# First block of a two-block transformer on one core: where half products, norms and turns stand in the order of the cycles

## The chip, the cores and the metric

The kernel runs on one core of one Trainium2 chip. The metric is the device time of one execution in microseconds (us); lower is better. A core has five engines that run in parallel, each through a queue of its own in order: TensorE (PE in the profile, with its weight loads as PEld), VectorE (DVE), ScalarE (ACT), GpSimd (POOL), and SyncE (SP), which here only issues DMA transfers. PE writes its results to PSUM, which has eight banks of 128 partitions by 512 floats. A second PE product can only go into a bank when the engine that reads the first one has read it.

## The reference, cut to what matters

Two transformer blocks follow each other on x of 8 batches, 512 tokens and 256 features, all in float32. The change touches the first block only:

```python
# 16 heads of 16 features, scale = 16 ** -0.5
h = modulate(ln(x), shift_sa, scale_sa)
q = ln(_heads(h, H)) * qn_w + qn_b
k = ln(_heads(h, H)) * kn_w + kn_b
v = _heads(h, H)
attn = softmax(q @ k.T * scale)                    # 512 x 512 for each head
x = x + gate_sa * unheads(attn @ v)
h = modulate(ln(x), shift_ca, scale_ca)
q = heads(h @ wq.T + bq)                           # keys and values from 64 context tokens
x = x + gate_ca * (unheads(softmax(q @ k.T * scale) @ v) @ ca_out_w.T + ca_out_b)
h = modulate(ln(x), shift_ff, scale_ff)
x = x + gate_ff * (silu(h @ w1.T) * (h @ w3.T)) @ w2.T   # 1024 hidden features
```

The second block (self-attention, cross-attention and a feed-forward with 64-wide heads) follows for all batches.

## The kernel before, in words

**Order by hand.** The first block is written with every engine's order fixed by the program: whatever a function emits stands in each engine's queue in the order of the calls. What differs from one build to the next is only which PSUM bank (`bank()`, L75, eight of them) a product gets.

**Stages and cycles.** Three classes hold the work of one batch: SelfAttention (`norm` L493, `centre`, `square`, `var`, `scale` L533 to L553, `heads_turned` L560, `queries_keys` L575, `score` L598, `value` L606, `back` L630), CrossAttention (`prepare` L677, `turn`, `blocks`, `queries` , `score` L705, `value` L712, `inverse` L726, `scaled` L729, `out` L734) and FeedForward (`prepare` L742, `up` L757, `down` L774). `beginning` (L797) runs batch 0's self-attention. Then `cycle(c)` (L841) runs for c = 1 to 7: self-attention of batch c (`s`), parts of the norm of batch c+1 (`nxt`), cross-attention of batch c-1 (`x`), the upper half of the feed-forward of batch c-2 (`up`), and the output product of cross-attention c-2 (`done`) and the lower half of feed-forward c-3 (`down`). `ending` (L875) finishes. In cycle 1 the keys of the second block's cross-attention (`keys1`, L929) are computed beside it, two rounds of products for each pair.

**Groups.** A cycle has four groups of self-attention, g = 0 to 3, of four heads each, and one of cross-attention between groups 2 and 3. `group` (L787) puts them in order:

```python
for fn in (*scores[:2], *beside, *scores[2:], *short, *values, *rest):
    fn()
```

A score for one block of 128 keys is four matmuls of 16 rows, one in each quarter of the PE array, so that they can run at the same time; each writes a bank of its own. ACT takes the exponentials (L655) into `p` tiles, of which there are 14; a group needs 16. The values are sixteen matmuls that add up in one bank. So a pair of scores fills all eight banks, and the next products wait for exponentials.

**Turns.** Queries and keys need the heads along partitions, and the values have to come back to tokens. There are two ways for both. On PE: four transposes against the identity (L591 for queries and keys, L638 in `back`), after ACT has copied the values from their bank (L625). By blocks: DVE transposes blocks of 32 by 32 (L564 in `heads_turned`, L617 in `value`, L413 in `blocks_turned`) and DMA writes the blocks to DRAM and reads them back in order (L567 to L572: six transfers; L621 to L623: five). `by_blocks` (L627) chooses for the values: every batch but the first, and not the last group of the last batch.

**Norms.** `norm(0)` and `norm(1)` take the statistics of two of four tiles each on DVE and end with a power on POOL (L158); `norm(2)` scales four tiles on DVE (L191, `ln`) and modulates them on POOL (L509, L511). `inverse` (L727) is one reciprocal of 128 by 512 on DVE, `scaled` (L731) multiplies with it and also calls `check` (L125), two reductions that only watch the range of numbers.

## Time and profile before

| what | value |
|---|---|
| runs | 2304.17 us median (2301.11 to 2304.48) |
| profiled execution, own time | 2307.33 us |
| its span | 2305.5 us |
| mean granted clock of PE | 0.989 |
| PE, DVE, ACT, POOL busy | 2269.9, 1161.9, 849.9, 883.2 us |
| cycle 1, first scores to the next cycle's first scores | 78.46 to 152.67 us |
| cycles 2, 3, 4 | from 152.67, 239.97, 331.67 us |
| cycle 7, to its last values | 605.05 to 693.39 us |

The span is that of the instructions on the core; the time of an execution includes what lies around it. A line of the timeline gives start, length, engine, line, operation, tiles (written<-read) and count, and in brackets the idle time ahead with what ended it. PE counts one float32 matmul as two records, a transpose as one. Line numbers are those of the kernel before; `ps_B` is a bank of the first block, L88 the helper through which all matmuls go. PEclk is the share of PE's full clock that was granted.

Of the kernel before, what the change touches and what calls it, by code (L numbers as in the profile page):

```python
# [10 lines left out]
F32 = mybir.dt.float32  # L11
# [33 lines left out]
def fast_path(ctx: ExitStack, tc: tile.TileContext, a: dict, out: bass.AP):  # L45
# [437 lines left out]
    class SelfAttention:  # L483
# [143 lines left out]
        def by_blocks(self, g):  # L627
            return self.b > 0 and (self.b, g) != (B - 1, 3)
# [43 lines left out]
    class CrossAttention:  # L672
# [56 lines left out]
        def scaled(self, c):  # L729
            s = self.s  # L730
            nc.vector.tensor_tensor(s["oT", c], s["oT", c], s["den", c], ALU.mult)  # L731
            check(s["den", c])
# [4 lines left out]
    class FeedForward:  # L737
# [19 lines left out]
        def up(self, f):  # L757
            s = self.s
            if f == 0:
                s["hid"] = wk3.tile([P, 8, N], F32, tag="hid", name="hid", bufs=1)  # L760
            fs = slice(f * P, (f + 1) * P)
            pss = []
            for w in (w_1, w_3):
                ps = bank()
                for k in range(2):
                    mm(ps, w[:, k, fs], s["hT"][:, k, :], k == 0, k == 1)
                pss.append(ps)

            t = wk3.tile([P, N], F32, tag="t", name="t")
            nc.scalar.activation(t, pss[0], AF.Tanh, scale=0.5)  # L770
            nc.vector.scalar_tensor_tensor(t, t, 1.0, pss[0], ALU.add, ALU.mult)
            nc.vector.tensor_tensor(s["hid"][:, f, :], pss[1], t, ALU.mult)

        def down(self, qp):  # L774
            project_out(qp, lambda k: self.s["hid"][:, k, :], w_2, 8, add_gated(wk2, self.b, self.s["gate"]))

# [64 lines left out]
    def cycle(c):  # L841
# [4 lines left out]
        keys = [lambda p=p: keys1(p) for p in range(NPAIR)] if c == 1 else [lambda: None] * NPAIR  # L846
        store = store_keys1 if c == 1 else lambda g: None
        late = [up.turn] if c == 2 else []
        soon, then = ([x.turn], []) if c == 1 else ([], [x.turn])
        rows2, rows3 = ([] if c < n else [s.blocks] for s, n in ((x, 2), (up, 3)))  # L850

        scores, values = of_self(s, 0)
        group(scores, [keys[0], keys[1], lambda: done.out(0), lambda: done.out(1), lambda: up.prepare(0), lambda: up.prepare(1),
                       lambda: down.down(0), lambda: up.prepare(2), *rows3],
              [lambda: s.queries_keys(1), lambda: prev.back(3), lambda: nxt.norm(0), lambda: nxt.norm(1)], values, late)
        scores, values = of_self(s, 1)
        group(scores, [keys[2], lambda: store(0), lambda: s.heads_turned(1), lambda: down.down(1), lambda: x.prepare(0),
                       lambda: x.prepare(1), *([up.turn] if c > 2 else []), lambda: up.up(0), lambda: x.prepare(2), keys[3],
                       lambda: up.up(1), *rows2],
              [lambda: s.queries_keys(2), lambda: s.back(0), *soon, lambda: nxt.norm(2)], values)  # L860
        scores, values = of_self(s, 2)
        group(scores, [keys[4], *then, lambda: store(1), lambda: up.up(2), lambda: nxt.centre(0), lambda: up.up(3),
                       lambda: nxt.square(0), lambda: x.queries(0), lambda: x.queries(1)],
              [lambda: s.queries_keys(3), lambda: s.back(1), lambda: nxt.var(0), lambda: nxt.scale(0)], values)
        group([lambda: x.score(0), lambda: x.score(1)],
              [keys[5], lambda: up.up(4), keys[6], lambda: up.up(5), lambda: s.back(2), lambda: nxt.heads_turned(0),
               lambda: nxt.centre(1)], [], [lambda: x.value(0), lambda: x.value(1)])
        scores, values = of_self(s, 3)
        group(scores, [keys[7], lambda: store(2), lambda: x.inverse(0), lambda: up.up(6), lambda: x.scaled(0), lambda: nxt.square(1),
                       lambda: up.up(7)],  # L870
# [1501 lines left out]
```

### The profile page before, as it was taken

To read this page: it belongs to the slowest core of one execution; us is meant where nothing else is said; L and a number is where in the kernel's file an instruction comes from. 1 tells how busy PE (TensorE), PEld (TensorE's weight loads), DVE (VectorE), ACT (ScalarE), POOL (GpSimd) and SP (SyncE) were. 2 spreads that over 40 slices of the span, in tenths; PEclk is the share of its full clock that TensorE was granted. 3 is DMA by queue.
4 is the path that set the end of the run, shared out by engine and by line. 5 is a ranking of instruction groups with operands and counts; after the bars stand their busy time and mean duration, and the time that the engine had idled before them with its cause. 6 is when DMAs were issued, how large, how long until landed. Compare 5 with 4: busy or idle time off the path is not lost.

```text
span 2305.5 us, 30615 instructions
## 1 busy us (share of the span) xinstructions
PE 2269.9 (98%) x11880; PEld 1130.7 (49%) x11880; DVE 1161.9 (50%) x2018; ACT 849.9 (37%) x1282; POOL 883.2 (38%) x552
## 2 busy tenths in 40 slices
PE   9899999999999999999999999999999899999999
PEld 4333544535535543444444444444445456567666
DVE  5765765666555535444444445454444666642220
ACT  4555455464552123333333333333332121321221
POOL 4553333233211036555454545454544433320110
PEclk9999999999999999999999999999999999999999
DMA  6233313223220201111111111111032445442221
GB/s 192 56 110 97 76 47 87 75 50 89 58 68 31 66 1 46 26 29 29 29 29 29 29 29 29 29 26 32 20 88 83 105 104 121 93 102 56 56 62 36
DMA packets 148586, 139.62 MB, mean 61 GB/s; under 512 B 41009, under 2 KB 115489, under 8 KB 148433
## 3 DMA queue, kind: packets, MB, share of 16 engines
q1 hardware_dynamic: 147568, 134.96, 23.2%
q8 instruction: 95, 1.56, 0.3%
q0 software_dynamic: 576, 2.10, 0.2%
q10 hardware_dynamic: 288, 0.52, 0.1%
q14 instruction: 59, 0.48, 0.1%
HBM read 99.19 MB, written 38.35 MB: 60 GB/s over the span
## 4 chain that ended last, share of the span: by engine, by line
PE 91%; DVE 4%; DMA 3%; issue 1%; POOL 1%; SPq 1%; ACT 0%; DVEq 0%; POOLq 0%; ACTq 0%
PE ps_P L88 41%; PE ps_B L88 30%; PE ps_X L88 7%; PE ps_S L88 6%; PE ps_D L88 5%; PE ps_O L88 3%; DMA rb<-rec 1%; DMA turned_d<-hT 1%; DMA rec<-rec 0%; DVE p L1379 0%; DVE z L191 0%; DVE ln L191 0%; POOL var L557 0%; DVE t L911 0%; DVE hT L413 0%
## 5 line engine op out<-in xcount | busy, mean ns | idle before, releaser
L655 ACT ACTIVATE p<-ps_B 128x512 f32<-128x512 f32 x576 | 290.6, 629 | 201.9 <-PE ps_B L88 201.8
L1102 ACT ACTIVATE p<-ps_P 128x1024 f32<-128x1024 f32 x256 | 244.8, 1025 | 89.4 <-PE ps_P L88 89.4
L88 PE MATMUL ps_P<-q,k 32*128 32x512 f32 x2048 | 238.9, 600 | 1.4 <-DVE t L1081 1.4
L88 PE MATMUL ps_B<-hT,w 128*128 128x512 f32 x512 | 230.1, 604 | 0.9 <-ACT hT L407 0.9
L1111 POOL TENSOR_TENSOR sm<-sm,p 128x1024 f32<-128x1024 f32 x64 | 177.2, 2769 | 135.1 <-ACT p L1102 134.4
L88 PE MATMUL ps_P<-p,v 128*32 128x512 f32 x2048 | 226.4, 594 | 0.0
L158 POOL TENSOR_TENSOR rstd<-rstd,mhalf 128x4 f32<-128x4 f32 x49 | 52.4, 1069 | 325.9 <-DVE rstd L157 324.5
L1111 DVE TENSOR_TENSOR sm<-sm,p 128x1024 f32<-128x1024 f32 x64 | 102.0, 1594 | 145.0 <-ACT p L1102 145.0
L1070 ACT COPY v<-ps_P 128x1024 f32<-128x1024 f32 x32 | 32.4, 1012 | 377.0 <-PE ps_P L88 377.0
L88 PE MATMUL ps_B<-q,k 16*128 16x512 f32 x1024 | 156.1, 620 | 11.8 <-DVE oT L617 10.4
L88 PEld LDWEIGHTS ps_P<-q,k 32*128 32x128 f32 x2048 | 99.1, 184 | 139.2 <-issue 113.6
L88 PEld LDWEIGHTS ps_B<-hT,w 128*128 128x128 f32 x512 | 96.4, 192 | 129.1 <-issue 101.4
L88 PEld LDWEIGHTS ps_P<-p,v 128*32 128x32 f32 x2048 | 63.3, 110 | 158.3 <-issue 134.8
L557 POOL TENSOR_TENSOR var<-var,mhalf 128x32 f32<-128x32 f32 (+1 forms) x17 | 87.8, 5162 | 132.9 <-DVE var L551 132.9
L1109 POOL TENSOR_TENSOR sm<-p 128x1024 f32<-128x1024 f32 x32 | 79.1, 2471 | 152.7 <-ACT p L1102 152.7
L1080 DVE TENSOR_TENSOR t<-ps_P,rope_c 128x1024 f32<-128x1024 f32 x64 | 78.4, 1225 | 106.7 <-POOL q L1084 64.5
L88 PE MATMUL ps_B<-p,h 128*32 128x512 f32 x1024 | 131.7, 596 | 0.0
L1109 DVE TENSOR_TENSOR sm<-p 128x1024 f32<-128x1024 f32 x32 | 39.2, 1225 | 171.9 <-ACT p L1102 171.9
L88 PE MATMUL ps_P<-hT,w_sa_wq 128*128 128x512 f32 x256 | 118.4, 605 | 0.8 <-issue 0.8
L88 PE MATMUL ps_B<-w,hid 128*128 128x256 f32 x512 | 118.2, 391 | 0.0
L88 PE MATMUL ps_P<-hT,w_sa_wk 128*128 128x512 f32 x256 | 115.1, 592 | 0.0
L88 PE MATMUL ps_P<-w_sa_wv,hT 128*128 128x512 f32 x256 | 114.9, 592 | 0.0
(253 smaller groups left out, 3553.9 us busy)
## 6 DMA issues: line engine op xcount, KB each, us to landing
z<-turned_d SPq DMA_DIRECT2D x35, 512.0 KB
rb<-rec_d SPq DMA_DIRECT2D x64, 256.0 KB
rb<-rec SPq DMA_DIRECT2D x32, 512.0 KB
turned_d<-hT SPq DMA_DIRECT2D x104, 128.0 KB
back_d<-oT SPq DMA_DIRECT2D x108, 64.0 KB
oT<-back_d SPq DMA_DIRECT2D x27, 256.0 KB
turned_d<-sm SPq DMA_DIRECT2D x36, 128.0 KB
out_dram<-x SPq DMA_DIRECT2D x15, 256.0 KB
```

The costliest lines, as they stand in the source:

```text
L88: nc.tensor.matmul(o, lhsT, rhs, start=start, stop=stop)
L158: nc.gpsimd.tensor_tensor(r[:, :n], r[:, :n], mhalf[:, :n], ALU.pow)
L557: nc.gpsimd.tensor_tensor(var, var, half, ALU.pow)
L655: nc.scalar.activation(p[i], ps, AF.Exp, scale=HD0 ** -0.5)
L1070: nc.scalar.copy(s["v", half][:, t0 : t0 + 2, :], ps)
L1080: nc.vector.tensor_tensor(c, ps, rope_c[:, None, :].to_broadcast([P, 2, N]), ALU.mult)
L1102: nc.scalar.activation(pr, pss[u], AF.Exp, scale=HD1 ** -0.5)
L1109: eng.tensor_tensor(s["sm", g, u], s["p", g, 0, u], s["p", g, 1, u], ALU.add)
L1111: eng.tensor_tensor(s["sm", g, u], s["sm", g, u], s["p", g, kt, u], ALU.add)
```

## The change

Cycle 1 gets a list of its own without feed-forward work. In it batch 1's values and the queries and keys of groups 2 and 3, and of batch 2's groups 0 and 1, are turned on PE: `by_blocks` now begins with batch 2, and the two `heads_turned` of cycle 1 are gone. x.turn stays in group 1, and var(1) and scale(1) of batch 2 stay in group 3.

In the other cycles:
- `up` is split into gate_half (w_1, tanh, product on DVE) and value_half (w_3 and the last product). The value half of up(1) and of up(7) moves between second scores and values.
- down(0) becomes two tiles: the first stands directly behind the first scores of group 0, the second between second scores and values. Each has its own product with the gate and sum, 128 by 256.
- x.queries(1) moves between second scores and values of group 2.
- norm(0) and norm(1) (group 0), norm(2) (group 1), var(0) and scale(0) (group 2) move from ahead of the values to behind them.
- inverse(1) of cross-attention moves from group 3 to the next cycle's group 0, behind the first scores; scaled(1) follows the first tile of down, then var(1) and scale(1), then out(0) and out(1). The checks are taken out of `scaled` into `checked` and stand behind up.prepare(1).
- In cycle 7 inverse(1), scaled(1) and the checks stand behind the last values.

```diff
         def by_blocks(self, g):
-            return self.b > 0 and (self.b, g) != (B - 1, 3)
+            return self.b > 1 and (self.b, g) != (B - 1, 3)
...
         def scaled(self, c):
             s = self.s
             nc.vector.tensor_tensor(s["oT", c], s["oT", c], s["den", c], ALU.mult)
-            check(s["den", c])
+
+        def checked(self, c):
+            check(self.s["den", c])
...
         def up(self, f):
+            self.gate_half(f)
+            self.value_half(f)
+
+        def half(self, f, w):
+            ps = bank()
+            for k in range(2):
+                mm(ps, w[:, k, f * P : (f + 1) * P], self.s["hT"][:, k, :], k == 0, k == 1)
+            return ps
+
+        def gate_half(self, f):
             s = self.s
...
+            ps = self.half(f, w_1)
+            s["t"] = t = wk3.tile([P, N], F32, tag="t", name="t")
+            nc.scalar.activation(t, ps, AF.Tanh, scale=0.5)
+            nc.vector.scalar_tensor_tensor(t, t, 1.0, ps, ALU.add, ALU.mult)
+
+        def value_half(self, f):
+            s = self.s
+            nc.vector.tensor_tensor(s["hid"][:, f, :], self.half(f, w_3), s["t"], ALU.mult)
...
+        def down_tile(self, t):
+            ps = bank()
+            project_tile(ps, 0, lambda k: self.s["hid"][:, k, :], w_2, 8, t)
+            tmp = wk2.tile([P, 2, D], F32, tag="tmp", name="tmp", bufs=1)
+            x = xs[self.b][:, t, :]
+            nc.vector.tensor_tensor(tmp[:, 0, :], ps[:, 0:D], self.s["gate"], ALU.mult)
+            nc.vector.tensor_tensor(x, x, tmp[:, 0, :], ALU.add)
...
+        if c == 1:
+            scores, values = of_self(s, 0)
+            group(scores, [keys[0], keys[1]],
+                  [lambda: s.queries_keys(1), lambda: prev.back(3), lambda: nxt.norm(0), lambda: nxt.norm(1)], values)
+            scores, values = of_self(s, 1)
+            group(scores, [keys[2], lambda: store(0), lambda: x.prepare(0), lambda: x.prepare(1), lambda: x.prepare(2), keys[3]],
+                  [lambda: s.queries_keys(2), lambda: s.back(0), x.turn, lambda: nxt.norm(2)], values)
+            scores, values = of_self(s, 2)
+            group(scores, [keys[4], lambda: store(1), lambda: x.queries(0), lambda: x.queries(1)],
+                  [lambda: s.queries_keys(3), lambda: s.back(1), lambda: nxt.centre(0)], values)
+            group([lambda: x.score(0), lambda: x.score(1)],
+                  [keys[5], lambda: nxt.square(0), keys[6], lambda: s.back(2), lambda: nxt.var(0), lambda: nxt.scale(0),
+                   lambda: nxt.centre(1)], [], [lambda: x.value(0), lambda: x.value(1)])
+            scores, values = of_self(s, 3)
+            group(scores, [keys[7], lambda: store(2), lambda: x.inverse(0), lambda: x.scaled(0), lambda: x.checked(0),
+                           lambda: nxt.square(1)],
+                  [lambda: nxt.queries_keys(0), lambda: x.inverse(1), lambda: x.scaled(1), lambda: x.checked(1),
+                   lambda: nxt.var(1), lambda: nxt.scale(1)], values)
+            store(3)
+            return
         scores, values = of_self(s, 0)
+        early = [] if c == 2 else [lambda: done.inverse(1)]
+        group(scores, [*early, lambda: down.down_tile(0), *([] if c == 2 else [lambda: done.scaled(1)]),
+                       *([] if c == 2 else [lambda: s.var(1), lambda: s.scale(1)]),
+                       lambda: done.out(0), lambda: done.out(1), lambda: up.prepare(0), lambda: up.prepare(1),
+                       *([] if c == 2 else [lambda: done.checked(0), lambda: done.checked(1)]), lambda: up.prepare(2), *rows3],
+              [lambda: s.queries_keys(1), lambda: down.down_tile(1), lambda: prev.back(3)], values,
+              [lambda: nxt.norm(0), lambda: nxt.norm(1), *late])
         scores, values = of_self(s, 1)
+        group(scores, [lambda: s.heads_turned(1), lambda: down.down(1), lambda: x.prepare(0),
+                       lambda: x.prepare(1), *([up.turn] if c > 2 else []), lambda: up.up(0), lambda: x.prepare(2),
+                       lambda: up.gate_half(1), *rows2],
+              [lambda: s.queries_keys(2), lambda: up.value_half(1), lambda: s.back(0)], values, [lambda: nxt.norm(2)])
         scores, values = of_self(s, 2)
+        group(scores, [x.turn, lambda: up.up(2), lambda: nxt.centre(0), lambda: up.up(3),
+                       lambda: nxt.square(0), lambda: x.queries(0)],
+              [lambda: x.queries(1), lambda: s.queries_keys(3), lambda: s.back(1)], values,
+              [lambda: nxt.var(0), lambda: nxt.scale(0)])
...
         scores, values = of_self(s, 3)
+        group(scores, [lambda: x.inverse(0), lambda: up.up(6), lambda: x.scaled(0), lambda: nxt.square(1), lambda: up.gate_half(7)],
+              [lambda: nxt.queries_keys(0), lambda: up.value_half(7)], values)
+        if s.b == B - 1:
+            x.inverse(1)
+            x.scaled(1)
+            x.checked(0)
+            x.checked(1)
```

## The prediction

> **What bounds the kernel now.** First the busy shares of the page and TensorE's (PE's) waits:
>
> ```profile
> PE 2269.9 (98%) x11880; PEld 1130.7 (49%) x11880; DVE 1161.9 (50%) x2018; ACT 849.9 (37%) x1282; POOL 883.2 (38%) x552
> ...
> PE ps_B L88 <- DVE oT L617: 10.4, 7, 5.0
> PE ps_B L406 <- DVE z L191: 4.8, 2, 3.8
> ```
>
> PE is the bound: it is idle for only 35.6 of 2305.5 us. Time comes from waits, from matmuls that run at half clock, or from packed matmuls that lose their packing. The largest wait is for L617, VectorE's (DVE's) transpose of a group's values: the next scores need the bank it reads. Next cycle 1 in the timelines (start us, length us, engine, line, operation):
>
> ```profile
> 108.98 1.99 PE L88 MATMUL ps_B<-q,k 16*128 16x512 f32 x14
> 115.99 2.07 PE L88 MATMUL ps_B<-q,k 16*128 16x512 f32 x2 [5.02 <-DVE oT L617]
> 118.00 3.78 PE L88 MATMUL ps_B<-ctxzT,w_ck 96*128 96x512 f32 x4
> ...
> 109.69 5.63 DVE L191 TENSOR_SCALAR ln<-x,mv,rstd 128x256 f32<-128x256 f32 x4
> 115.23 0.70 DVE L617 STREAM_TRANSPOSE oT<-ps_B 128x512 f32<-128x512 f32 x1
> ```
>
> The norm's four `ln` (norm(2)) stand ahead of L617. The scores take 9.02 us from 108.98 to 118.00 where 1.93 is usual. Then the turn of cycle 4 to 5:
>
> ```profile
> 419.64 3.75 PE L88 MATMUL ps_B<-p,h 128*32 128x512 f32 x32
> 423.31 2.99 PE L88 MATMUL ps_B<-q,k 16*128 16x512 f32 x16
> 426.23 3.72 PE L88 MATMUL ps_B<-w_o,oT 128*128 128x256 f32 x16
> 436.79 2.00 PE L88 MATMUL ps_B<-q,k 16*128 16x512 f32 x16
> 438.72 4.35 PE L88 MATMUL ps_B<-p,h 128*32 128x512 f32 x32
> 445.51 1.12 PE L88 MATMUL ps_B<-q,k 16*128 16x512 f32 x2 [0.51 <-DVE oT L617]
> ...
> 444.74 0.72 DVE L617 STREAM_TRANSPOSE oT<-ps_B 128x512 f32<-128x512 f32 x1
> ```
>
> From start to start a pair of scores costs 1.93 us (436.79 to 438.72). When its last matmul comes too late to run beside its three neighbours the pair costs about 1 us more (423.31 to 426.23 is 2.92), with no idle shown. Values cost 3.67 (419.64 to 423.31), but 4.3 where they run right behind the second scores, whose exponentials ScalarE (ACT) still works on. Cycle 4 runs from 353.05 to 443.00, 89.95 us. It loses 0.99 at its first scores, 0.61+0.67+0.64 at three sets of values, 1.62 at group 0 to 1, 0.60 in group 3: 5.1 in all.
>
> Last the clock (stretch, us, busy of PE, PEld, DVE, ACT, POOL, PEclk, DMA):
>
> ```profile
> 51.43:54.85 3.42, 3.42 (x8) 1.18 (x10) 0.00 (x0) 2.42 (x5) 3.34 (x2) 0.50 0.00 0
> 58.26:61.67 3.41, 3.41 (x34) 0.96 (x32) 3.27 (x10) 1.49 (x3) 1.14 (x2) 1.00 0.00 0
> 259.65:263.06 3.41, 2.90 (x17) 1.00 (x16) 2.98 (x11) 2.18 (x5) 2.17 (x3) 1.00 0.58 111
> 263.06:266.47 3.41, 3.41 (x8) 2.52 (x8) 0.00 (x0) 2.23 (x5) 0.00 (x0) 0.50 0.99 295
> 112.87:123.11 10.24, 7.12 (x8) 2.69 (x9) 4.29 (x6) 1.46 (x3) 8.97 (x7) 0.50 0.28 74
> 78.46:152.67 74.21, 67.44 (x361) 25.03 (x361) 44.90 (x95) 41.25 (x80) 40.61 (x29) 0.91 0.24 68
> ```
>
> Scores with a wait of 0.52 us (259.65) are followed by 3.41 us at half clock: 1.7 us lost; so are bare scores (48.02 to 51.43, then 51.43 at 0.50). Cycle 1 takes 74.2 us at a mean clock of 0.91.
>
> **The change, cycle 1 (gain).** The block turns through DMA become PE turns: queries_keys(2), (3), and (0), (1) of the next batch, four sets of 0.49 (89.28 to 89.77 in cycle 1); back(0) to back(3) of batch 1, four of 0.53 (89.77 to 90.30). That adds 4.1 us of PE work, 3.1 in cycle 1 and 1.0 in cycle 2, and takes 4 L617, 2 L564 and 32 DMA issues away (5 for each L617, 6 for each L564); their SP queue then holds little else, so the gate that POOL waited 6.1 us for at 109.34 comes early. The bank is now freed by ACT's copy (0.585, L625), which waits behind no norm; ACT is busy 41 of 74 us here and has the room (were it full, 0.6 would stand ahead of a score). I step through the new order with these rows:
> - Group 0 ends as before (93.9). In group 1 the first scores lose their 0.41, the second still lose 1; x.turn waits some 0.9 for `t` of keys 3 (now 1.07); values end at 109.1.
> - Group 2's scores start at once: the 7.09, and the 1.77+0.77 that the next products lose to the half clock, are gone. q and k from PSUM cost 0.8 each, now 0.55 (+0.5). Group 2 ends at 122.9, the cross group (1.93+3.53+0.53+3.57) at 132.5.
> - Group 3: second scores end at 138.7; the added turn for nxt.queries_keys(0) waits for POOL's scaling of `z` (var at 131.5, pow 5.44, product 1.06: 139.7). Values end at 143.8, `k` comes at 144.3, behind keys 7 1.2, inverse 3.38, scaled 0.61, check 1.18.
>
> So cycle 1 takes 144.3-78.5 = 65.8, now 74.2: **-8.4**.
>
> **Cycle 2 (gain).** Its out(0) still waits for inverse(1) on DVE (3.35+0.69 behind `k`; 156.65 now). L617 of group 0 loses norm(0), norm(1) (2.06 us, 170.17 to 172.23), but up.turn, still behind the values, now waits for `z`: POOL's pow(5.44)+1.06+rstd stands before it. About even. In group 1 norm(2) (4.63 at 187.37) leaves the place ahead of L617: 1.65 idle and 1.0 of lost packing go, and the half clock of 194.8 (1.7). I take **-4**.
>
> **Cycles 3 to 7 (loss).** Here the same products move, and I count what waits.
> - First scores of group 0: inverse(1) no longer stands ahead of L617: -0.99. But the DVE order is now L617, inverse(1) 3.38, down_tile(0)'s product 0.45 and sum 0.42, scaled(1). The tile ends on PE 1.93+3.5 = 5.43 after the cycle's start, scaled(1) at 7.07; out(0)'s second matmul, due at 5.86, stands until 7.1: +1.25. PE's queue holds the second scores and values behind it; were scaled(1) ahead of the tile's product, this wait would be nil.
> - DVE's further chain: var 0.92, out(1)'s product at 10.3 and sum 1.34, stats 2.1, checks 2x1.18, `z` 1.41, transpose 1.17, q and k 0.88, tile 0.87, back(3) 0.99: L617 starts at 21.4. Now it starts at 444.74-423.31 = 21.4 too: norms 2.06 left, inverse and checks came in. The values end at 19.3 and do save 0.61, but group 1's last score waits as now. Group 0 to 1: 23.15 against 23.25, **-0.1**. Cycle 7 has no norm now and no loss there (605.05 to 626.67 is 21.62): **+1.5**.
> - gate_half ahead of second scores: the last score needs DVE's product on the gate bank, which needs tanh (0.6+0.68+latency, 1.5 behind the gate's matmuls; due at 0.98). Group 1 loses 0.7 and saves 0.67 on values; group 3 loses 0.57, now 0.60. In group 2 the last score needs the first query's conversion (12.5 after the group's start, due at 11.6): +1.0-0.64. Together **+0.4** a cycle.
>
> A cycle changes by +0.3, four of them +1.2; cycle 7 +1.9; at its end inverse(1) behind value_half delays out(0) by 0.6. Half-clock stretches: three now (263, 335, 447: 5.1 us); the stretch of bare scores at group 0 to 1 is about as long (3.85, now 3.6), so I expect two, **-1.5**. A group has 16 exponentials and 14 buffers for them: the last two wait on ACT until the first values, now behind the inserted product, free two; they end 2.1 into the values, the last values need them at 2.75, and ACT's next work (the next exponentials) is later still. Edits of equal work (down as two tiles: DVE +0.3 a cycle in its gaps; checks moved, store and keys no-ops) cost nothing while DVE has idle, as at 429 to 437; inside the chain they are counted.
>
> Sum: -8.4-4+1.2+1.9+0.6-1.5 = **-10.2** of the profiled 2305.5. I give back 2 for waits that I could not see in cycles 1 and 2 (bounds: 0, and a half-clock stretch each plus 1, so 5): -8.2. The runs' median, 2304.17, lies 1.3 below the span; 2296.
>
> **Rules against rows.** The Trainium skill, "TensorE: Matmul & The Clock Gate", Part 4 (PE-mode transpose), says that transposes don't count as PE activity for the clock. That speaks against this change: eight sets beside scores would make two or three more half-clock stretches, +3 to +5, and the sum would be -4. But from 54.85 to 58.26 scores stand with 0.94 us of turns and nothing else, and the clock behind it is 1.00 (58.26), while scores beside 0.5 us of products (48.02 to 51.43) lost it. I go by the row. Part 1 (the HAM clock gate) of that page says an idle window of about 3.4 us brings half clock; by that, waits of 0.5 to 1.7 us cost none, and cycle 2 would gain 1.7 less. Row 263.06 decides: 0.50.
>
> **Rivals.**
> - *Cycles 3 to 7 gain too.* If the late last scores overlap with the products that follow, group losses of 0.7, 1.0 and 0.57 vanish: 5 times 2 is 10 more, 2286. For: the 0.61 to 0.67 on values is real. Against: 423.31 shows a late last score not overlapped.
> - *It gives the gain back.* inverse(1) and scaled(1) around the tile: if the 1.25 wait and the longer stretch of scores at group 0 to 1 take a half-clock stretch each in most cycles (+1.7 to +3.4), five cycles cost 8.5 to 17 more: 2305 to 2313, slower. It decides above 3.3 a cycle. Against: beside 1.25 us idle stand 2.1 us of full products in a window, and 536.13 (1.3 full, 0.5 idle) kept its clock.
> - *Turns cost what DMA waits did.* PE turns wait for banks, `z` and POOL in groups 1 and 3 of cycle 1 and up.turn in cycle 2: 6 of the 12 gone, 2302, same. For: POOL's pow of 5.44 stands before two of them.
>
> **How the numbers follow.** Forecast (2290 to 2299) 0.47, first rival 0.15, second 0.17, third 0.21. What a measurement tells from no change is 0.2%, 4.6 us: 2299.6 to 2308.8. Faster: 0.47+0.15 = 0.62; same: 0.21 and a fifth of the second rival above, 0.24; slower 0.14. Range 2284 to 2308 leaves 0.2 out.
>
> **What would show it.** Cycle 1 at 64 to 68 us with no wait for oT; a wait of PE for oT L731 of about 1.2 in each of cycles 3 to 7; last scores late in groups 1 to 3; L617 of group 0 still 21 to 22 behind the cycle's start. Wrong, if PE's order of out(0) does not wait for scaled(1), if packing is not lost, or if clock drops follow the turns.

## The result: 0.22% slower, and the profile after

The changed kernel takes 2311.1 us (median, 2306.57 to 2315.98) against 2306.0 (2301.11 to 2312.63) of the kernel before on the same chip: a ratio of 1.0022, with a 95% interval of 1.0013 to 1.0032. Forecast was 2296, a gain. The profiled execution took 2308.91 us over a span of 2307.0.

The page's busy shares, and the waits of PE (us in total, times, longest):

```profile
PE 2265.4 (98%) x11912; PEld 1125.4 (49%) x11912; DVE 1159.0 (50%) x2022; ACT 854.5 (37%) x1286; POOL 883.5 (38%) x552
```

```profile
PE ps_B L88 <- DVE oT L731: 7.8, 7, 1.4
...
PE ps_B L88 <- DVE k L585: 4.4, 5, 0.9
PE ps_B L88 <- DVE oT L617: 3.9, 6, 1.7
```

The wait of 5.0 us in cycle 1 is gone, and the waits for L617 fall from 10.4 to 3.9. But `scaled` (L731) and `k` (L585) now hold PE up in every one of cycles 3 to 7. PE is busy for 4.5 us less than before and the kernel is longer.

The timeline of PE in cycle 1, where the wait of 5.02 stood, and over the start of cycle 5:

```profile
105.45 2.00 PE L88 MATMUL ps_B<-q,k 16*128 16x512 f32 x16
107.38 1.98 PE L88 MATMUL ps_B<-ctxzT,w_ck 96*128 96x512 f32 x4
...
136.39 0.66 PE L591 MATMUL ps_B<-ident,z 128*128 128x128 f32 x4 [0.98 <-POOL z L558]
```

```profile
414.87 2.10 PE L88 MATMUL ps_B<-q,k 16*128 16x512 f32 x16
416.91 3.72 PE L88 MATMUL ps_B<-w,hid 128*128 128x256 f32 x16
420.47 0.59 PE L88 MATMUL ps_B<-w_o,oT 128*128 128x256 f32 x2
422.21 3.29 PE L88 MATMUL ps_B<-w_o,oT 128*128 128x256 f32 x14 [1.15 <-DVE oT L731]
425.43 2.00 PE L88 MATMUL ps_B<-q,k 16*128 16x512 f32 x16
427.36 3.72 PE L88 MATMUL ps_B<-w,hid 128*128 128x256 f32 x16
431.01 3.64 PE L88 MATMUL ps_B<-p,h 128*32 128x512 f32 x32
435.53 1.99 PE L88 MATMUL ps_B<-q,k 16*128 16x512 f32 x14 [0.88 <-DVE k L585]
437.96 1.12 PE L88 MATMUL ps_B<-q,k 16*128 16x512 f32 x2 [0.44 <-DVE oT L617]
```

The transpose that its last line waits for, in the timeline of DVE:

```profile
437.19 0.72 DVE L617 STREAM_TRANSPOSE oT<-ps_B 128x512 f32<-128x512 f32 x1
```

Group 2 of cycle 1 starts its scores at once (105.45 to 107.38 is 1.93). Cycle 1 takes 64.8 us (76.07 to 140.84) in place of 74.2, cycle 2 83.8 in place of 87.3; at the start of cycle 3 the changed kernel stands 15.3 us ahead (224.67 against 239.97). Of these, 2.4 are not due to the change: its cycle 1 starts at 76.07 and not at 78.46, because the half-clock window that before has ahead of cycle 1 (51.43 to 54.85) did not occur in this execution. All profiles without such a window start cycle 1 at 75.5 to 76.2, whatever their order, and those with one at 78.2 to 78.5. The second block of lines shows how the lead is lost in each of the later cycles: 1.15 at out(0), 0.88 for `k`, 0.44 for the transpose. From the end of the values (434.65) to the next full product (439.01, down(1)) PE does nothing but scores and waiting for 4.36 us.

The stretches (us, busy of PE, PEld, DVE, ACT, POOL, PEclk, DMA share, GB/s) of cycles 3 to 6, first of the changed kernel, then of the kernel before, and the clock around one such place:

```profile
224.67:602.98 378.31, 368.17 (x1829) 171.79 (x1825) 231.83 (x496) 189.96 (x360) 119.00 (x76) 0.97 0.26 68
340.08:343.50 3.42, 2.66 (x16) 1.00 (x16) 3.32 (x13) 1.88 (x4) 1.37 (x2) 1.00 0.79 152
343.50:346.91 3.41, 3.41 (x8) 2.19 (x7) 1.77 (x7) 2.15 (x5) 1.11 (x2) 0.50 0.55 144
```

```profile
239.97:605.05 365.08, 363.03 (x1825) 173.38 (x1824) 231.14 (x489) 188.39 (x360) 118.75 (x76) 0.99 0.28 71
```

The four cycles take 378.3 us, before 365.1: 13.2 of the 15.3 are given back. The stretch of scores at group 0 to 1 is followed by half clock in every one of cycles 3 to 7, at 247.9, 343.5, 439.1, 531.2 and 626.8, for 6.8 or 3.4 us each, 27.3 us in all; before there were three of 3.4. The mean clock over the span hides it (0.990, before 0.989), because cycles 1 and 2 have 6.8 us of half clock in this execution and 23.9 in that of before. That is in good part a draw of windows: in the profile of filled (below), whose cycles 1 and 2 are the same, it is 20.5.

### The profile page after: what moved, and what is told of

Read it like the earlier page. It is cut to its first block, busy times and chain, and to the rows that moved or that the text cites. A ratio compares the mean times of both kernels' runs of the same rounds, so it can differ in the third digit from the quotient of the medians.

```text
span 2307.0 us, 30635 instructions
## 1 busy us (share of the span) xinstructions
PE 2265.4 (98%) x11912; PEld 1125.4 (49%) x11912; DVE 1159.0 (50%) x2022; ACT 854.5 (37%) x1286; POOL 883.5 (38%) x552
## 4 chain that ended last, share of the span: by engine, by line
PE 89%; DVE 6%; DMA 1%; POOL 1%; issue 1%; SPq 0%; ACT 0%; DVEq 0%; POOLq 0%; ACTq 0%
PE ps_P L88 41%; PE ps_B L88 27%; PE ps_X L88 7%; PE ps_S L88 6%; PE ps_D L88 5%; PE ps_O L88 3%; DVE z L191 1%; DMA rb<-rec 1%; DVE st L182 1%; POOL var L557 1%; DVE chk L129 1%; DVE den L727 0%; DVE tmp L471 0%; DVE attn L647 0%; DVE x L473 0%
## 5 line engine op out<-in xcount | busy, mean ns | idle before, releaser
L88 PE MATMUL ps_B<-w,hid 128*128 128x256 f32 x512 | 127.3, 410 | 0.0
L88 PEld LDWEIGHTS ps_B<-w,hid 128*128 128x128 f32 x512 | 104.5, 207 | 29.8 <-ACT p L655 13.4
L88 PE MATMUL ps_B<-p,h 128*32 128x512 f32 x1024 | 117.0, 595 | 0.0
```

Source lines behind the costliest of these rows:

```text
L88: nc.tensor.matmul(o, lhsT, rhs, start=start, stop=stop)
```

## The experiments

All start from the changed kernel unless said otherwise, and compute everything. "Stretch" is PE's time from the end of group 0's values (or of the product that an experiment puts behind them) to the next full product, where the clock was full; "cycle" is the length of a cycle from 3 to 6 at full clock (of one without half clock; for before, changed, cycle1_alone, rest_alone, norms_ahead and whole_halves of one with it, less half of the half-clock time); "half" is the half-clock time in cycles 3 to 7 of the profiled execution. The clock's windows lie differently in every execution, so "half" is one draw, and times are medians. Each ratio is to runs of before beside that experiment (medians 2305.2 to 2306.9).

| kernel | stretch | cycle | half | median | ratio to before, 95% |
|---|---|---|---|---|---|
| before | 3.48 | 89.95 | 10.2 | 2306.0 | |
| changed | 4.36 | 91.33 | 27.3 | 2311.1 | 1.0013 to 1.0032 |
| cycle1_alone | 3.48 | 90.0 | 13.7 | 2297.3 | 0.9940 to 0.9972 |
| rest_alone | 4.4 | 91.3 | 30.7 | 2325.9 | 1.0060 to 1.0101 |
| norms_ahead | 7.3 | 93.2 | 37.5 | 2324.4 | 1.0066 to 1.0101 |
| scaled_first | 3.87 | 89.42 | 20.5 | 2292.2 | 0.9912 to 0.9954 |
| checks_later | 3.2 | 90.17 | 17.1 | 2294.1 | 0.9927 to 0.9968 |
| both | 3.87 | 89.42 | 6.8 | 2291.9 | 0.9922 to 0.9954 |
| inverse_back | 3.88 | 90.31 | 13.7 | 2304.9 | 0.9981 to 1.0006 |
| whole_halves | 4.36 | 90.74 | 17.1 | 2300.9 | 0.9970 to 0.9988 |
| var_back | 3.6 | 90.57 | 23.9 | 2306.2 | 0.9988 to 1.0011 |
| tile_behind | 3.16 | 90.85 | 6.8 | 2298.6 | 0.9942 to 0.9975 |
| filled | 2.44 | 91.33 | 0 | 2296.8 | 0.9939 to 0.9972 |
| both_tile_behind | 2.67 | 88.93 | 0 | 2285.2 | 0.9892 to 0.9929 |
| both_tile_whole | 2.67 | 88.35 | 0 | 2283.4 | 0.9878 to 0.9918 |
| both_var_back | 2.44 | 88.00 | 0 | 2281.5 | 0.9872 to 0.9908 |
| tile_whole_var | 1.86 | 87.54 | 0 | 2274.4 | 0.9840 to 0.9880 |
| both_whole_var | 2.44 | 87.41 | 0 | 2272.2 | 0.9833 to 0.9872 |

### The two halves of the change: cycle1_alone, rest_alone

```diff
# cycle1_alone: cycle 1's own list is kept, the list of the other cycles is that of before
# rest_alone: the list of before for c == 1 (turns by blocks), the rest as changed
-            return self.b > 1 and (self.b, g) != (B - 1, 3)
+            return self.b > 0 and (self.b, g) != (B - 1, 3)
```

> The change's cycle 1 (turns on PE) with cycles 2 to 7 in the order of before. Theory (the loss lies in the new order of cycles 3 to 7): cycle 1 takes 64.8 us as in the changed kernel, nothing is given back, 2306.0 - 9.4 = 2295 to 2298, with half clock in three or four places of cycles 3 to 7. Rival (the earlier start of cycle 2 only shifts the work against the clock's windows, and the loss follows from the shift): cycles 3 to 7 show a half-clock stretch each here too, 2302 to 2306.

> Cycle 1 as before (turns by blocks and DMA), cycles 2 to 7 and their end as in the change. Theory: cycle 2 gains about 3, cycles 3 to 7 lose 3.4 each, which makes +14 on 2306.0, 2318 to 2322. Rival (shift against the clock's windows): the cycles of the new order lose only their waits, 1.15 + 0.9 + 0.4 less what values save, 2306 to 2311.

cycle1_alone took 2297.3: the turns on PE in cycle 1 gain 7.9 by the medians, and nothing of it is given back. Its profiled execution, at 2303.25 the slowest of ten, missed the expected 64.8 for cycle 1. The stretches of cycle 1 in the changed kernel and in cycle1_alone (this one starts 0.5 us ahead of the first scores):

```profile
76.07:140.84 64.77, 62.61 (x385) 25.01 (x385) 41.71 (x90) 42.98 (x84) 41.07 (x29) 1.00 0.12 39
```

```profile
77.97:146.93 68.96, 66.59 (x384) 26.74 (x384) 42.23 (x91) 42.97 (x84) 41.09 (x29) 0.93 0.13 38
```

The same program for cycle 1 takes 64.8 us at full clock and 68.4 with three windows at half clock. Of the sixteen profiles with the new cycle 1, six have 64.8 and ten 67.5 to 69.4. So the 9.4 us between the traces of before and after are a good draw; the 7.9 of the medians is the safer figure.

rest_alone took 2325.9, above the theory's 2318 to 2322. Its cycles 3 to 6 take 377.3 us, as in the changed kernel (378.3), so the loss belongs to their order and not to where cycle 1 ends. What was too low in the expectation is cycle 2: I counted a gain of 3 there, and it took 86.9 us (before 87.3, changed 83.8): with cycle 1 as before, the new cycle 2 waits 1.20 for `k` and 2.53 for L617. The two halves therefore don't add up to the change (-7.9 and +20.7 against +5.1): cycle 2 gains only behind the new cycle 1. In the profiles that is 3.1 of the 7.7 us between sum and change; the rest was not traced.

### Does a longer stretch cost what it adds, or the clock: filled

```diff
+        def again(self):
+            ps = bank()
+            for k in range(4):
+                mm(ps[:, 0:D], self.s["hid"][:, k, 0:P], w_2[:, k, :], k == 0, k == 3)
...
-              [lambda: nxt.norm(0), lambda: nxt.norm(1), *late])
+              [down.again, lambda: nxt.norm(0), lambda: nxt.norm(1), *late])
```

> The changed kernel with work added: behind the values of group 0 in cycles 3 to 7 TensorE repeats half of a down tile (four products of 128 by 256, 1.8 us) into a bank that nothing reads. Nothing else moves. Theory (half clock follows windows in which scores stand nearly alone; the waits of 0.88 and 0.44 are the DVE chain's): the added work fills the wait for k and most of the wait for the transpose, so a cycle without half clock is longer by 0.4 to 0.9 only, and half clock at that place goes in all or nearly all cycles: -5 to -10 against the changed kernel, 2301 to 2306, although PE does 9 us more. Rival (half clock comes from elsewhere): +4 to +9, 2315 to 2320.

2296.8: with 1.9 us of useless products added to each of five cycles (9.6 in all) the kernel is 14.3 us faster, more than the theory's 5 to 10. PE's timeline at group 0 to 1 of cycle 5, and cycles 3 to 6 as a whole:

```profile
426.96 3.64 PE L88 MATMUL ps_B<-p,h 128*32 128x512 f32 x32
430.53 1.99 PE L88 MATMUL ps_B<-w,hid 128*128 128x256 f32 x8
432.45 2.58 PE L88 MATMUL ps_B<-q,k 16*128 16x512 f32 x16
434.97 7.17 PE L88 MATMUL ps_B<-w,hid 128*128 128x256 f32 x32
```

```profile
228.05:593.49 365.44, 360.74 (x1861) 170.52 (x1857) 235.73 (x496) 189.96 (x360) 119.07 (x76) 1.00 0.27 71
```

The added products stand where PE waited for `k`; values, products and scores together take 8.0 us (426.96 to 434.97), as values, waits and scores do in the changed kernel (431.01 to 439.01). A cycle takes 91.33 us, what the changed kernel's would take at full clock. What differs is the half clock, which is gone (1.00 over the four cycles): it costs the changed kernel about 14 us.

### What makes the stretch long: norms_ahead, scaled_first, checks_later, both, inverse_back, var_back

```diff
# norms_ahead: norm(0), norm(1), norm(2), var(0), scale(0) ahead of the values again
-              [lambda: nxt.norm(0), lambda: nxt.norm(1), *late])
+              late)
# scaled_first
-        group(scores, [*early, lambda: down.down_tile(0), *([] if c == 2 else [lambda: done.scaled(1)]),
+        group(scores, [*early, *([] if c == 2 else [lambda: done.scaled(1)]), lambda: down.down_tile(0),
# checks_later: to the end of group 1, behind norm(2)
-                       *([] if c == 2 else [lambda: done.checked(0), lambda: done.checked(1)]), lambda: up.prepare(2), *rows3],
+                       lambda: up.prepare(2), *rows3],
# inverse_back: to group 3, ahead of the values, and gone from group 0; the checks stay
-              [lambda: nxt.queries_keys(0), lambda: up.value_half(7)], values)
+              [lambda: nxt.queries_keys(0), lambda: up.value_half(7), lambda: x.inverse(1), lambda: x.scaled(1)], values)
# var_back: to group 3, behind the values, and gone from group 0
-              [lambda: nxt.queries_keys(0), lambda: up.value_half(7)], values)
+              [lambda: nxt.queries_keys(0), lambda: up.value_half(7)], values, [lambda: nxt.var(1), lambda: nxt.scale(1)])
```

> The changed kernel with norm(0), norm(1), norm(2), var(0) and scale(0) back ahead of the values in cycles 2 to 7. Theory (the DVE chain of group 0 sets the stretch of scores): norm(0) and norm(1), 2.06 us, stand ahead of the transpose again, the scores at group 0 to 1 take 5 to 6 in place of 3.5: +1.5 to +2 a cycle, half clock of 6.8 in every cycle, cycle 2 loses 3: 2320 to 2328. Rival (DVE has room there): 2309 to 2313.

> The changed kernel with scaled(1) ahead of the first tile's two DVE operations in cycles 3 to 7, so that the second matmul pair of out(0) has what it needs. The 1.15 us wait goes in five cycles. Theory (the wait costs only its own length; the half clock comes from the bare scores at group 0 to 1): -5, 2305 to 2307, half clock still in every cycle. Rival (the wait is what drops the clock): -5 and -8 more, 2297 to 2299, half clock gone in most cycles.

> The changed kernel with the two checks (four DVE reductions, 2.4 us) moved from group 0 to the end of group 1 in cycles 3 to 7. Theory (the DVE chain of group 0 delays k and L617, and the longer stretch of scores drops the clock): k and L617 2.4 us earlier, the waits of 0.88 and 0.44 go, the scores at group 0 to 1 take 2 to 3 instead of 3.8, and half clock stays in at most two or three cycles: -6 to -15, 2296 to 2305. Rival (the halves with their late last scores, or the 1.15 wait, cost the cycles): -1 to -5 at most and half clock in every cycle, 2306 to 2310.

> scaled(1) ahead of the first tile's DVE operations and the checks at the end of group 1, both. The wait of 1.15 is gone, k and the transpose of group 0 wait for nothing, and scores at group 0 to 1 stand some 3 us without a full product. Theory (waits add up, a shorter stretch of bare scores falls more seldom on a whole clock window): cycles of 89.0 to 89.4 without half clock, at most two half-clock stretches in cycles 3 to 7, 2284 to 2290. Rival (both edits cure the same thing): as scaled_first, 2291 to 2294.

> The changed kernel with inverse(1) and scaled(1) of cross-attention back in group 3, ahead of the values, as before the change; the checks stay in group 0. Theory (inverse(1) in group 0 makes both the 1.15 us wait and, with the checks, the late k): the 1.15 and the 0.88 go, the first scores of the next cycle lose some 0.9 again, so -1 to -1.5 a cycle, and half clock in about half of the cycles instead of all: 2296 to 2303. Rival (halves and late last scores are the cause): 2308 to 2312.

> The changed kernel with var(1) and scale(1) of the self-attention behind the values of group 3, one cycle part earlier than in the change, so that POOL's power of 5.4 us and product of 1.1 us no longer stand in group 0. Theory (they are part of why the transpose came 0.9 later than predicted: the rstd operation of 0.93 in place of 0.17 is VectorE held up by POOL's product): that operation takes 0.17, the wait for k shrinks from 0.88 to about 0.1, a cycle without half clock takes 90.3 to 90.7 in place of 91.3, -3 to -5 and half clock in fewer cycles, together 2295 to 2303. Rival (the 0.76 is something else, the chain is set by inverse(1) and the checks alone): 2307 to 2311.

norms_ahead, 2324.4, is as expected; that part of the change helps in the new order. The last matmul of group 1's first scores there (two records), in PE's timeline:

```profile
450.62 2.07 PE L88 MATMUL ps_B<-q,k 16*128 16x512 f32 x2 [2.47 <-DVE oT L617]
```

scaled_first, 2292.2, beats both of its expectations. Not 1.15 us a cycle goes with the wait but 1.9 (91.33 to 89.42): the products of out(0) and out(1), the statistics and `k` all stand behind that wait on DVE and move up with it, and one operation of this chain, the norm's L157, gets shorter by 0.76. That one takes longer in the changed kernel (0.17 us before, in cycles 3 to 7). The timelines of DVE and of POOL in the changed kernel, and of DVE in scaled_first:

```profile
428.72 0.93 DVE L157 TENSOR_SCALAR rstd<-mv 128x4 f32<-128x4 f32 x1
429.56 2.45 DVE L129 TENSOR_REDUCE chk<-den 128x1 f32<-128x512 f32 x4
```

```profile
428.56 1.06 POOL L558 TENSOR_TENSOR z<-z,var 128x512 f32<-128x512 f32 x1
```

```profile
420.14 0.17 DVE L157 TENSOR_SCALAR rstd<-mv 128x4 f32<-128x4 f32 x1
```

It ends together with POOL's L558, in cycles 3 to 7 alike. Where the chain runs ahead of L558 (scaled_first) or L558 is in another place (var_back) it takes 0.17. So scale(1), which the change moved into group 0, holds DVE up; the Trainium skill, "SBUF — State Buffer", Terms, says that DVE and GpSimd share a pair of ports and that the loser of it stands still for the whole of the other's instruction, which fits the row.

checks_later took 2294.1, a little under the theory's range, and its stretch is 3.2. It should add to scaled_first; but in both (2291.9) cycle and stretch are those of scaled_first, as the rival had it. DVE in both, at `z` of the feed-forward's norm, and then in both_var_back (below), where var(1) and scale(1) stand in group 3:

```profile
425.05 1.38 DVE L191 TENSOR_SCALAR z<-x,mv,rstd 128x256 f32<-128x256 f32 x4 [2.54 <-POOL rstd L158]
```

```profile
419.74 1.38 DVE L191 TENSOR_SCALAR z<-x,mv,rstd 128x256 f32<-128x256 f32 x4 [1.12 <-POOL rstd L158]
```

With the checks gone DVE waits in their place: POOL's rstd stands behind its power of 5.44 us for var(1). So there were three ties on `k` and L617, one behind the other: scaled(1), the checks, and POOL's work for var(1). ("Tie" is meant here for a dependence that holds the chain back.)

inverse_back (2304.9) and var_back (2306.2) shorten the cycle by 1.0 and 0.8, as expected (91.33 to 90.31 and 90.57), 5 and 4 us over five cycles. That is nearly all of their gain of 6.2 and 4.9 in the medians: both theories had the half clock go in part, and neither time shows it. The profile of inverse_back, with half of the changed kernel's half clock, is the fastest of 14 executions (2298.16; the slowest took 2312.98). Their stretches (3.88, 3.6) are no longer than that of both (3.87), which gains 19.2 with 9.6 of it by its cycle. I come back to this below.

### The halves: whole_halves

```diff
-                       lambda: up.gate_half(1), *rows2],
-              [lambda: s.queries_keys(2), lambda: up.value_half(1), lambda: s.back(0)], values, [lambda: nxt.norm(2)])
+                       lambda: up.up(1), *rows2],
+              [lambda: s.queries_keys(2), lambda: s.back(0)], values, [lambda: nxt.norm(2)])
# likewise up(7) and x.queries(1)
```

> The changed kernel with up(1), up(7) and the second query whole and ahead of the second scores again. Theory (a late last score costs 0.6 to 0.8, the values save as much, each split product costs 0.2): -0.4 a cycle, the half clock at group 0 to 1 unchanged in cycles 3 to 7: 2307 to 2311. Rival (late last scores of groups 1 to 3 cost the cycles): -2 a cycle and fewer half-clock stretches, 2295 to 2303.

2300.9, under the theory's range (2307 to 2311) and within the rival's (2295 to 2303), but not by the rival's mechanism: the cycle is 0.6 shorter (90.74), not 2, and the half clock comes in every cycle at group 0 to 1 with a stretch of the same 4.36. What is less is that each lasts one window, where three of the changed kernel's five last two. The five windows at half clock:

```profile
247.02:250.43 3.41, 3.41 (x10) 2.66 (x9) 0.64 (x2) 0.98 (x3) 1.02 (x1) 0.50 0.64 187
339.18:342.59 3.41, 3.41 (x9) 2.70 (x9) 0.88 (x3) 1.25 (x3) 1.02 (x1) 0.50 0.70 212
431.34:434.75 3.41, 3.41 (x9) 2.70 (x9) 1.14 (x5) 1.52 (x4) 1.02 (x1) 0.50 0.71 200
523.50:526.91 3.41, 3.41 (x9) 2.75 (x9) 1.41 (x6) 1.79 (x4) 1.02 (x1) 0.50 0.57 152
615.66:619.07 3.41, 3.41 (x8) 2.40 (x8) 0.00 (x0) 2.02 (x5) 0.00 (x0) 0.50 0.57 174
```

They are 92.16 us apart, 27 windows of 3.413. A cycle of 90.74 that loses 1.7 takes 92.43, nearly a multiple of the window, so the stretch meets the window in the same place in the next cycle and drops the clock again. inverse_back (90.31 + 1.7 = 92.0), var_back (92.27) and checks_later (91.9) are as near to 27 windows; both and scaled_first (91.1) and the kernel before (91.65, or 89.95 without) are less so. This fits what the seven did, but cycle length was not varied by itself, so it stays an argument.

### From this to a faster kernel: tile_behind and its combinations

```diff
# tile_behind
-              [lambda: s.queries_keys(1), lambda: down.down_tile(1), lambda: prev.back(3)], values,
-              [lambda: nxt.norm(0), lambda: nxt.norm(1), *late])
+              [lambda: s.queries_keys(1), lambda: prev.back(3)], values,
+              [lambda: down.down_tile(1), lambda: nxt.norm(0), lambda: nxt.norm(1), *late])
# both_tile_behind = scaled_first + checks_later + tile_behind;  both_tile_whole: + whole_halves
# both_var_back = scaled_first + checks_later + var_back;  both_whole_var: + whole_halves
# tile_whole_var = both_whole_var + tile_behind
```

> The changed kernel with the second tile of down behind the values of group 0 in cycles 3 to 7, so that full products stand between those values and the next scores. Theory (the stretch of bare scores and waits at group 0 to 1, 4.4 us long in the changed kernel, is what the half clock follows): no half clock at that place in any cycle; without it the cycle is 1 to 1.7 us shorter (k wait 0.9 and late scores 1.4 gone, values 0.6 longer right behind the scores): -18 to -22, 2289 to 2293. Rival (the half clock follows the 1.15 us wait of out(0) or the late last scores of the halves): half clock goes on, -5 to -8, 2303 to 2306.

> scaled(1) first, the checks at the end of group 1, and the second tile of down behind the values of group 0. Theory: k is ready when the tile ends, scores at group 0 to 1 take 2.0 to 2.5 and stand alone for less than 2.7, so no window drops there: cycles of 88.3 to 88.6 (both: 89.4) and no half clock in cycles 3 to 7 but a rare one at the second scores of group 1: 2279 to 2285. Rival (the second tile behind the values costs what it saves, as values lengthen by 0.6 and the last score waits for the tile's product): cycles of 89.4 to 90, 2288 to 2293.

> As both_tile_behind, and up(1), up(7) and the second query whole again. Theory (each split costs 0.2 in its products and 0.1 in the next first scores and gains nothing over its late last score): 0.5 to 0.6 less a cycle, no second scores of 2.7 that a window can drop on: 2276 to 2283. Rival (halves save on values what they cost): equal to both_tile_behind within 1.

> scaled(1) first, checks at the end of group 1, and var(1), scale(1) behind the values of group 3. In the kernel with the first two edits VectorE stands idle for 2.5 us until POOL's rstd, which runs behind POOL's power for var(1). Theory (that power now sets k and the transpose of group 0): rstd comes 1.5 earlier, the waits of 0.39 and 0.44 go, scores at group 0 to 1 take 2.0 to 2.5, cycles of 88.0 to 88.4 (89.4 with the first two edits alone), hardly a half-clock stretch: 2279 to 2286. Rival (POOL's chain has other cover): 2290 to 2293.

> As both_var_back with up(1), up(7) and the second query whole: 0.5 to 0.6 a cycle less, cycles of 87.4 to 87.9, 2276 to 2283. Rival (the halves give slack at group 3 that var(1) now needs): 2283 to 2288.

> As both_whole_var with the second tile of down behind the values. Theory: its scores at group 0 to 1, 2.74 with var(1) in group 0, wait for less and take 2.0 to 2.3, but the values stand right behind second scores and take 0.6 longer: cycles of 87.7 to 88.0, 2278 to 2283, no half clock in cycles 3 to 7. Rival (the tile's product on VectorE holds the last score, not POOL): cycles of 88.4 as in both_tile_whole, 2282 to 2284.

tile_behind, 2298.6, falls between the two. The wait of 1.15 for L731 is still there and the half clock nearly gone (6.8 in place of 27.3), which excludes that wait as its cause; but two cycles dropped, where I expected none: the scores still stood alone for 3.0 us (341.39 to 344.38 in cycle 4): the last of them start at 343.33, just behind the tile's product on DVE, which ends at 343.28. both_tile_behind (2285.2, the upper end of the theory's range) brings the stretch to 2.67 and no cycle drops; both_tile_whole shortens the cycle by the expected 0.6; its median is 1.8 lower, which the spread of the times (2276.9 to 2284.0, against 2281.2 to 2288.0) does not make sure. both_var_back (2281.5) is as the theory had it: without POOL's power in group 0 both waits at group 0 to 1 go and a cycle takes 88.00.

both_whole_var is the fastest, 2272.2, 1.5% less than before and below its range, with the cycle as expected (87.41). tile_whole_var (2274.4, cycles of 87.54) is below its range too, and is not told apart from it. PE of both_whole_var at the turn of cycle 4 to 5, and its cycles 3 to 6:

```profile
404.61 2.00 PE L88 MATMUL ps_B<-q,k 16*128 16x512 f32 x16
406.54 3.72 PE L88 MATMUL ps_B<-w,hid 128*128 128x256 f32 x16
410.10 3.62 PE L88 MATMUL ps_B<-w_o,oT 128*128 128x256 f32 x16
413.64 2.12 PE L88 MATMUL ps_B<-q,k 16*128 16x512 f32 x16
415.69 3.72 PE L88 MATMUL ps_B<-w,hid 128*128 128x256 f32 x16
419.34 3.64 PE L88 MATMUL ps_B<-p,h 128*32 128x512 f32 x32
422.91 2.61 PE L88 MATMUL ps_B<-q,k 16*128 16x512 f32 x16
```

```profile
228.05:579.57 351.52, 350.06 (x1825) 167.28 (x1825) 236.42 (x496) 188.69 (x360) 119.31 (x76) 1.00 0.28 73
```

No wait stands in these lines, and the same work that took the changed kernel 378.3 us takes 351.5. The half clock that is left ahead of cycle 7's end lies before cycle 3: 20.5 us in cycles 1 and 2 of this profile.

## Why the prediction was wrong

- **Cycle 1, -8.4: right.** -7.9 by the medians of cycle1_alone; the -9.4 of the trace is a draw without half clock. The wait for `t` of keys 3 (0.96, forecast 0.9) and the one for POOL's scaling of `z` (0.98) are where the stepping had put them.
- **Cycle 2, -4: right** (-3.5), with the wait for L617 at 1.68 "about even" (before 1.70). Not seen: it depends on cycle 1 (rest_alone). Cycles 1 and 2 together are the sounder figure: 161.5 us before, 148.6 here and 146.4 to 150.1 in the fourteen profiles that have the new order, or a variant of it, in both.
- **The wait of out(0) for scaled(1), 1.25: right in place and size** (1.15), and wrong in what hangs on it. That it would be nil with scaled(1) first was said; that DVE's products of out, the statistics and `k` come later with it was not followed to its end. scaled_first: 1.9 us a cycle and 18.9 us in all.
- **L617 21.4 us behind the cycle's start: this failed.** It came at 22.32 (437.19, the line of DVE above, less 414.87). From the checks to L617 the sum was right (7.68, measured 7.63). Ahead of them it lacked L157 (0.17 in the trace of before): with scale(1) moved in, POOL's product stands beside it and it took 0.93. The last score starts where this transpose ends (437.96), so group 0 to 1 took 24.14 us (414.87 to 439.01), not 23.15: +0.9 in place of **-0.1**. The 0.88 for `k` lies inside this and adds nothing: filled, without that wait, takes the same 24.14 (410.83 to 434.97).
- **Late last scores, +0.4 a cycle: the sum is right by luck.** Group 1's second scores cost 0.76 more (forecast 0.7), its values 0.77 less (0.67); group 2's 0.55 more (1.0) and 0.74 less (0.64). That makes -0.2. Only with 0.2 for each product split in two and 0.1 for first scores behind a last score so placed, neither of them in the forecast, do groups 1 to 3 lose 0.5. whole_halves gets 0.6 back.
- **Half clock "-1.5, I expect two instead of three": the step that decided.** It rested on "the stretch of bare scores at group 0 to 1 is about as long (3.85, now 3.6)". It was 4.36 (up to 5.3 where the clock fell within it), and every cycle dropped: +8.5 in the profiles (half of 27.3 less 10.2) in place of -1.5. filled prices the whole of it at 14.3 in the changed kernel. Nor were two drops sure for the length that was forecast: at stretches of 3.2 to 3.9 two of five cycles dropped at this place in both, three in inverse_back, four in checks_later and var_back. What decides among these was not tested (the 27 windows above are an argument).
- **End:** cycle 7 to its last values takes 4.4 more (92.7 us, 602.98 to 695.68, against 88.3), 1.7 of it half clock; forecast 1.9. The wait behind it was 0.57 (0.6).

By parts of the two traces: ahead of cycle 1 -2.4 (a draw); cycles 1 and 2 -12.9; cycles 3 to 6 +13.2; from cycle 7's start to the end of the span +3.6: +1.5 between the spans. Of the 16.8 us lost, the five cycles of +1.4 (91.33 against 89.95, forecast 0.3) make 7 and the half clock 8.5. The medians differ by +5.1; the lucky start of the changed kernel's profile would account for most of the rest, but only one execution of each was traced.

So the **second rival** is what happened: it named the longer stretch at group 0 to 1, and put the turn at 3.3 us a cycle; cycles 3 to 6 lose 3.3 on average. It had a wrong partner in it: the wait of 1.25 drops no clock (tile_behind and filled keep it), as "beside 1.25 us idle stand 2.1 us of full products" said. Its chance was too small: the stretch forecast, 3.85, was itself longer than a clock window of 3.41, and 0.5 us more were enough for a drop in every cycle.

**The rules weighed.** That transposes don't count for the clock (Part 4, as cited in the prediction) is not borne out. Two experiments have the same code up to here; their scores start at the same time, and the clock's windows lie 0.27 us apart. PE of tile_behind and its windows, then the same of inverse_back:

```profile
54.12 2.99 PE L88 MATMUL ps_B<-q,k 16*128 16x512 f32 x16
57.05 0.66 PE L591 MATMUL ps_B<-ident,z 128*128 128x128 f32 x4
```

```profile
54.29:57.70 3.41, 3.41 (x22) 1.53 (x23) 1.56 (x5) 3.07 (x6) 3.02 (x2) 1.00 0.00 0
57.70:61.11 3.41, 3.41 (x35) 1.16 (x34) 3.23 (x10) 1.78 (x4) 0.85 (x2) 1.00 0.00 0
```

```profile
53.12 1.04 PE L88 MATMUL ps_B<-kvT,wk 128*128 128x512 f32 x1
54.10 2.93 PE L88 MATMUL ps_B<-q,k 16*128 16x512 f32 x16
56.96 0.71 PE L591 MATMUL ps_B<-ident,z 128*128 128x128 f32 x4
```

```profile
54.02:57.44 3.42, 3.42 (x21) 1.49 (x21) 1.55 (x5) 2.96 (x6) 3.16 (x2) 1.00 0.00 0
57.44:60.85 3.41, 3.41 (x18) 1.27 (x20) 3.04 (x9) 1.31 (x3) 0.70 (x1) 0.50 0.00 0
```

With 0.65 us of turns in the window (57.05 to 57.70) and nothing else but scores the clock is kept. With 0.48 us of turns (56.96 to 57.44) and 0.08 us of a full product (54.02 to 54.10) it is lost, at no idle time in either. If turns did not count, the second window would be the one with more activity. At this place in eleven executions, the three windows with 0.55 us of turns and product lost the clock, and the eight with 0.65 to 0.99 us of turns alone kept it. That is where other products have their limit too (below). And an idle window of 3.4 us (Part 1) is not needed: the lost window had none. What the same part says of a free-running window agrees: its place against the program differs from execution to execution.

## What to carry to other kernels

When an operation moves into another engine's busy stretch, step through that engine and through what shares with it: here a chain 0.9 us late, with the half clock that the longer stretch of scores brought, turned a forecast gain of 0.4% into a loss of 0.2%. Ask of every place where PE has only low-row matmuls or waits whether it is as long as a clock window (3.4 us here): at group 0 to 1 no cycle with less than 2.7 us dropped, every one with more than 4 did, and between them two to four of five. A loop whose length is near a multiple of the window may repeat the drop each time (argued, not tested). Such a stretch is worth breaking up by any full product, even a useless one; best is to find which of several ties behind one another on the slack engine is the last, as curing the first two gave less than their sum. And compare two traces only after looking where each lost its clock: the same cycle 1 took 64.8 to 69.4 us.

## What the runs showed of the hardware that I had not expected

- **The clock follows activity, not idle time.** In the first 720 us of the eighteen profiles I took all clock windows at full clock in which PE never stood idle, and added up what was neither 16-row nor cross-attention scores (products, values, turns). From 0.45 to 0.85 us of it 38 were followed by half clock and about 40 were not; from 0.85 to 1.6 none of 668 was. Many of them are the same place in kernels that are alike there, so they count for less than their number. With idle time in the window the limit is higher: in the changed kernel a window with 1.36 us idle and 1.40 us of products (from 142.11) was followed by half clock.
- **More work, less time:** 9.6 us of added products, 14.3 us less.
- **DVE held by POOL:** a 128 by 4 operation took 0.93 us in place of 0.17 beside POOL's 128 by 512 product.
